# A GRU and an expert-choice layer on one core: units of the expert product twice as wide and in odd steps only, a block of the x products moved to even steps

## The chip, the core and the metric

The kernel runs on one core of one Trainium2 chip. The metric is the device time of one execution in microseconds; of several runs the median is taken. The profile is of one further execution of the same program.

## What is computed

A GRU runs over 256 steps on a batch of 16 with 512 channels. Its states are the tokens (16 x 256 = 4096) of an expert-choice layer: a router of 16 experts, a softmax, for each expert its 256 best tokens, and one weight matrix that all experts share. The result is added to `x`.

```python
def cell(h, x):
    gi = x @ W_ih + b_ih
    gh = h @ W_hh + b_hh
    i_r, i_z, i_n = jnp.split(gi, 3, axis=-1)
    h_r, h_z, h_n = jnp.split(gh, 3, axis=-1)
    r = jax.nn.sigmoid(i_r + h_r)
    z = jax.nn.sigmoid(i_z + h_z)
    n = jnp.tanh(i_n + r * h_n)
    return (1.0 - z) * n + z * h
# ffn over the states xf (4096 x 512), k = 4096 / 16 = 256
S = jax.nn.softmax(xf @ router_w + router_b, axis=-1)
G, idx = jax.lax.top_k(S.T, k)
out = jnp.einsum('ekh,hd->ekd', xf[idx], expert_w) + expert_b
y = zeros.at[idx].add(G[..., None] * out)
return x + y
```

Since the experts share a matrix, a token's output is its one row of `xf @ expert_w + expert_b` times the sum of the weights of those experts that chose it.

## The kernel before

**Tiling.** All matrix products are float32. TensorE is used as four strips of 32 columns: the 512 output channels are split over them (`tile_position=(0, 32 * j)`), and a loop over `j` issues four matmuls, one for each strip. Such a set of four is called a block here when it has 128 columns of the moving operand (32 channels x 4 chunks, or 128 channels of the expert matrix). In the trace each float32 matmul shows as two instructions, so a block is eight.

**The recurrence.** Loop `s` runs over the 256 steps; `p` is a pair of steps, `odd` the second of a pair, `g` a group of 8 steps and `c` the step in it. The order of instructions on all engines in this loop is the order in which the program writes them (a manual schedule). In a step TensorE does, in order:

1. `h_part` (L450 to L467): the products of the state with `W_hh`, for r and n over the first half of the channels, then over the second half, then for z. These wait for the state `hs`, whose two halves VectorE writes separately (L593). 12 blocks.
2. `x_part` (L436 to L448): the products of the pair after this one with `W_ih`, done for two steps at a time. For r and n together a matmul has 256 columns, for z 128. The even step does `k` 0 to 2 of r and n, the odd step `k` 3 of r and n and all four `k` of z. Each accumulates onto the bias that ScalarE has copied into the PSUM bank before.
3. An expert unit (L401 to L415): one block of one 128-column quarter of the expert product of an earlier group. There are 16 units in a group (4 quarters x 4 `k`), for the 15 `early_groups`; a counter lets one unit pass in each step from step 8 on. Or, in the first two steps of every fourth group (`apart`, steps 32 and 33, 64 and 65, up to 224 and 225), the router's `logits` of the four groups before (L336 to L351), into the right part of the bank `hn` of the next pair; the units left out follow in the step after.

Meanwhile ScalarE and VectorE work at the gates: sigmoid of r (L518), `t` = r x n part + i_n part (L568, L570), tanh (L572), sigmoid of z (L573), 32 x 32 transposes (L579, L582), and h = n + z (h - n) (L585, L590, L593).

**The bias copies of the next pair** are ScalarE's, in even steps. `preset_first` (L422) fills the bank `ra` right after r's sigmoid. `preset_rest` (L425) comes after z's sigmoid and fills `hn` (L426), in one pair of sixteen also clears the part for logits (L430), and then fills `zz` (L434).

**After the steps** TensorE still has the expert product of the 17 `late_groups`. It is cut into pieces by a generator, `late_parts` (L161 to L177), and `expert_for(n)` takes the next `n` of them wherever TensorE would wait: in the last two steps, after the last logits, in each of the 17 bits of the search for each expert's 256th largest weight (`by_bits`, L668: VectorE counts, a matmul adds up over partitions at L678, VectorE decides), and around what follows it. A piece is `late_part` (L133) over half of the 512 columns for one `k`, two blocks' worth; after the gate is known (`gated`) a piece is all 512 columns. What is left then is done in one go, and VectorE's `store` (L715) multiplies by the gate, adds `x` and sends the group out.

**Loads.** The weights come first on the queues of SyncE and ScalarE, the biases, the first `x` and `cond` on GpSimd's. `ewr` (expert and router matrix), `rb` (router bias, broadcast) and `eb` (expert bias, broadcast) follow on SyncE's (L296 to L299). `rb` is first read after the logits of step 33, `eb` in step 7.

Of the kernel before, what the change touches and what calls it, by code (L numbers as in the profile page):

```python
# [18 lines left out]
def kernel(  # L19
# [34 lines left out]
    nc = tc.nc  # L54
    B, T, D = x.shape
    E = router_w.shape[1]
    P = 128
    QD = 32
    KC = D // P
    TG = P // B  # L60
# [7 lines left out]
    HD = D // 2  # L68
    ewr = const.tile([P, KC, E + D], F32, name="ewr")
# [75 lines left out]
            )  # L145

    whole, halves_d = slice(0, D), [slice(0, HD), slice(HD, D)]

    late_items = [(g, whole) for g in late_groups[:-1]] + [(late_groups[-1], half) for half in halves_d]
    late = []  # L150
# [2 lines left out]
    gated = []  # L153
# [7 lines left out]
    def late_parts():  # L161
        for i, (g, cols) in enumerate(late_items):
            pe = late[0]
            for k in range(KC):

                for part in [cols] if gated or cols != whole else halves_d:
                    late_part(g, pe, k, part)
                    if k == KC - 1 and part.stop == cols.stop:
                        if i + 2 < len(late_items):
                            late_begin(ps_m if (i + 2) % 6 < 2 else late_pool[0])  # L170
                        late.pop(0)
                        late_done.append((g, cols))
                        if gated:
                            late_sums[g, cols.start] = pe
                        else:
                            nc.scalar.copy(wide(g), pe)
                    yield  # L177
# [4 lines left out]
    def expert_for(n):  # L182
        for _ in range(n):
            next(parts, None)


    with (
# [31 lines left out]
        def quadrant(j, m=QD):  # L219
            return slice(QD * j, QD * j + m)  # L220
# [44 lines left out]
        with tc.manual_schedule(engines={ET.SP, ET.Activation, ET.Pool}):  # L265
            def load_pairs(p, n, queue):

                for j in range(KC):
                    for i in range(n):
                        at = 2 * (p + i)  # L270
                        queue.dma_start(
                            out=xa0[quadrant(j), p + i, :],
                            in_=x[:, at : at + 2, j * P : (j + 1) * P].rearrange("b o d -> o b d"),
                        )

            for i, gate in enumerate((0, 2, 1)):
                load_rows(wih[:, :, i, :], w_ih[:, gate * D : (gate + 1) * D], "(p c) n -> p c n")
            for gate in (0, 2, 1):
                load_rows(whh[:, :, gate, :], w_hh[:, gate * D : (gate + 1) * D], "(c p) n -> p c n")

            for dst, src in (
                (b_raw[0:1], b_ih.rearrange("(o g d) -> o g d", o=1, d=D)),
                (b_raw[1:2], b_hh.rearrange("(o g d) -> o g d", o=1, d=D)),
                (b_n, b_hh[2 * D :].rearrange("(o d) -> o d", o=1)),
            ):
                nc.gpsimd.dma_start(out=dst, in_=src)
            load_pairs(0, 2, nc.gpsimd)
            nc.gpsimd.memset(c0, 0.0)
            for j in range(KC):
                nc.gpsimd.dma_start(  # L290
                    out=c0[QD * j : QD * j + B, :].rearrange("b (c i) -> b c i", c=KC), in_=columns(cond, j)
                )
            load_pairs(2, TG // 2 - 2, nc.sync)
            for j in range(KC):
                load_xa(1, xa1, j, (nc.sync, nc.sync))
            nc.sync.dma_start(out=ewr[:, :, E:], in_=expert_w.rearrange("(c p) n -> p c n", c=KC))  # L296
            nc.sync.dma_start(out=ewr[:, :, 0:E], in_=router_w.rearrange("(c p) n -> p c n", c=KC))
            nc.sync.dma_start(out=rb, in_=router_b.rearrange("(o e) -> o e", o=1).to_broadcast([P, E]))
            nc.sync.dma_start(out=eb, in_=expert_b.rearrange("(o d) -> o d", o=1).to_broadcast([P, D]))  # L299


# [51 lines left out]
        def last_logits(pl):  # L353

            j = KC - 1
            for k in range(KC):
                nc.tensor.matmul(
                    pl[quadrant(j, E)].rearrange("p (b t) -> p b t", t=TG)[:, :, TG - 1],
                    ewr[:, k, 0:E],
                    hs[:, k, slot(T), :],  # L360
                    start=False,
                    stop=(k == KC - 1),
                    tile_position=(0, QD * j),
                    skip_group_check=True,
                )

        def less_max(h, pl):
            l = gp.tile([P, KC, QD], F32, name="l")
# [26 lines left out]
        pes = {}  # L395
# [5 lines left out]
        def expert(g, unit):  # L401


            quarter, k = divmod(unit, KC)
            at = P * quarter
            for j in range(KC):
                nc.tensor.matmul(  # L407
                    pes[g][quadrant(j), at : at + P],
                    ht[:, g, k, quadrant(j)],
                    ewr[:, k, E + P * quarter : E + P * (quarter + 1)],  # L410
                    start=False,
                    stop=(k == KC - 1),
                    tile_position=(0, QD * j),
                    skip_group_check=True,
                )  # L415
# [9 lines left out]
        def preset_rest(p):  # L425
            nc.scalar.copy(hn[p % 2][:, 0:P], nb)  # L426


            if p % (KC * TG // 2) == TG + 1:
                nc.scalar.copy(  # L430
                    hn[p % 2][:, P:].rearrange("p (c e) -> p c e", e=QD),
                    zero.unsqueeze(1).to_broadcast([P, KC, QD]),
                )
            nc.scalar.copy(zz[p % 2], bias[:, 2, :])  # L434

        def x_part(p, k, z):  # L436
            g, pair = divmod(p, TG // 2)
            lhs = xT[g][:, pair, QD * k : QD * (k + 1)]
            for j in range(KC):
                q = quadrant(j)  # L440
                dst, rhs = (
                    (zz[p % 2][q], columns(wih[:, k, 2, :], j))
                    if z
                    else (ra[p % 2][q], columns(wih[:, k, 0:2, :].rearrange("p g d -> p (g d)"), j))
                )
                nc.tensor.matmul(  # L446
                    dst, lhs, rhs, start=False, stop=(k == KC - 1), tile_position=(0, QD * j), skip_group_check=True
                )  # L448
# [52 lines left out]

        with tc.manual_schedule(engines={ET.PE, ET.Activation, ET.DVE, ET.Pool, ET.SP}):
            seen = gp.tile([1, 8], F32, name="seen")
            units = [(g, unit) for g in early_groups for unit in range(16)]
            n_units = len(units)
            done = []
            for s in range(T):
# [20 lines left out]
                if 2 <= s < T - 2:  # L528
                    for k in range(3, KC) if odd else range(3):
                        x_part(p + 1, k, False)  # L530
                    if odd:
                        for k in range(KC):
                            x_part(p + 1, k, True)
                apart = g and g % KC == 0 and c < 2
                taken = done.pop(0) if done else None
                if apart:
                    logits(hn[(p + 1) % 2][:, P:], (2 * c, 2 * c + 1), range(g - KC, g))
                else:
                    while units and n_units - len(units) < s - TG + 1:
                        g_, unit = units.pop(0)  # L540
                        expert(g_, unit)
                        if unit == 15:
                            done += [(g_, 0), (g_, 1)]
                            break
                if s == T - 2:
# [1 line left out]
                if s == T - 1:  # L547
                    logits(hn[0][:, P:], range(KC), range(NG - 1, NG), slice(0, TG - 1))
                if s >= T - 2:
                    expert_for(1)  # L550

# [19 lines left out]
                nc.scalar.activation(zs, zz[p % 2], AF.Sigmoid)  # L573
                if not odd and 0 < p < T // 2 - 1:
                    preset_rest(p + 1)


                def turn_n(half):
# [57 lines left out]
            nc.vector.tensor_copy(  # L636
                ht[:, NG - 1, :, :].rearrange("p k (b t) -> p k b t", t=TG)[:, :, :, TG - 1], hs[:, :, slot(T), :]
            )
            expert_for(5)
            less_max(NG // KC - 1, hn[0][:, P:])  # L640
            for stage in range(4):
                softmax(slice(NG - KC, NG), stage)
# [2 lines left out]
    with (  # L645
# [85 lines left out]
        with tc.manual_schedule(engines={ET.PE, ET.Activation, ET.DVE}):  # L731
# [11 lines left out]
            nc.scalar.copy(by_block[:, 0 : KC - 1], ps[:, 0 : KC - 1, :].rearrange("p c (q i) -> p c q i", q=QG))  # L743
            nc.vector.tensor_copy(by_block[:, KC - 1], ps_last.rearrange("p (q i) -> p q i", q=QG))

            expert_for(2)
            counts = by_counts(HIGH - LOW + 1)
            top = by_bits(KNOWN, HIGH, LOW, counts, lambda bit: expert_for(3))


            nc.vector.scalar_tensor_tensor(at_least, sT, top.bitcast(F32), sT, ALU.is_le, ALU.mult)
# [6 lines left out]
                most.unsqueeze(1).to_broadcast([P, GH, NTOP]),  # L758
                ALU.mult,
            )  # L760
            expert_for(2)
            all_most = ps_n.tile([P, GH * NTOP], F32, name="all_most", tag="n")
            nc.tensor.matmul(all_most, same_f, spread.rearrange("p h n -> p (h n)"), start=True, stop=True)
            expert_for(3)
            room = above(counts)
            nc.vector.max(out=most, in_=all_most)
            kth = rt.tile([P, 1], F32, name="kth")
# [3 lines left out]
            for q in range(QG):  # L771
                part = slice(q * P, (q + 1) * P)
                nc.vector.scalar_tensor_tensor(at_least[:, part], sT[:, part], kth, sT[:, part], ALU.is_ge, ALU.mult)
                sum_weights(q, pg)
                if q % 2:
                    expert_for(1)
            gate = gate_of(pg)

            gated.append(True)
# [115 lines left out]
```

## Time and profile before

| | |
|---|---|
| median of 3 runs | 1161.14 us (1160.76 to 1162.51) |
| the profiled execution | 1161.04 us |
| its span, first to last instruction | 1159.2 us |
| granted TensorE clock, mean | 0.999 |
| TensorE busy | 1147.5 us, 99% |
| VectorE busy | 703.7 us, 61% |
| ScalarE busy | 343.4 us, 30% |
| first state product | 20.94 us |
| end of the last step | some 1087.8 us |
| gate ready, first store | some 1123.4 us |

In the rows of a timeline the first number is the start in us from the span's start, the second how long the row lasts; then the engine (PE TensorE's matmuls, PEld its weight loads, DVE VectorE, ACT ScalarE, POOL GpSimd, SP the queue of SyncE), the line of the kernel, the operation, what it writes and reads, the shape, and how many instructions are merged in the row. In brackets stands how long the engine was idle before, and what ended that.

### The profile page before, as it was taken

The numbers are of one execution on the slowest core, as the hardware profiler recorded it, in microseconds if no ns is written. First come the engines' busy times: TensorE is split into PE (matmuls) and PEld (weight loads), VectorE is DVE, ScalarE is ACT, GpSimd is POOL, SyncE is SP. The second block draws the span as 40 slices with busy tenths as digits, with TensorE's granted clock in tenths as the row PEclk, the third lists the DMA queues.
The fourth block names the chain that finished last, engine by engine and source line by source line (L and its number), as shares of the span: only waits on it lengthen the run. The fifth ranks groups of instructions, "written<-read, shape, count | busy, mean of one in ns | idle before, by whom it ended". The sixth has DMA issues, their size and how long they took to land. (4 is left out here: it accounts for less than half of the span.)

```text
span 1159.2 us, 79459 instructions
## 1 busy us (share of the span) xinstructions
PE 1147.5 (99%) x36065; PEld 1010.1 (87%) x36065; DVE 703.7 (61%) x4078; ACT 343.4 (30%) x1459; POOL 99.7 (9%) x412
## 2 busy tenths in 40 slices
PE   8999999999999999999999999999999999999998
PEld 5899999999999989999999999999999999989742
DVE  2656665666666656666665656666656666666675
ACT  1323323332233323333232323233232322343320
POOL 3000010000000000000000000000000000000000
PEclk9999999999999999999999999999999999999999
DMA  7200000000000000000000000000000000000017
GB/s 235 76 21 20 20 19 22 21 20 19 21 22 21 18 21 20 20 21 20 21 20 21 20 21 18 23 20 20 18 23 21 20 19 20 20 19 13 3 49 246
DMA packets 48855, 38.03 MB, mean 33 GB/s; under 512 B 7968, under 2 KB 40800, under 8 KB 48512
## 3 DMA queue, kind: packets, MB, share of 16 engines
q1 hardware_dynamic: 46272, 29.56, 8.7%
q8 instruction: 284, 4.65, 1.7%
q10 hardware_dynamic: 1632, 3.15, 0.8%
q14 instruction: 59, 0.48, 0.1%
q0 software_dynamic: 608, 0.19, 0.1%
HBM read 24.47 MB, written 8.39 MB: 28 GB/s over the span
## 5 line engine op out<-in xcount | busy, mean ns | idle before, releaser
L459 PE MATMUL gates<-whh,hs 128*16 128x128 f32 x24576 | 719.8, 273 | 3.4 <-DVE zT L582 1.2
L459 PEld LDWEIGHTS gates<-whh,hs 128*16 128x16 f32 x24576 | 672.4, 103 | 9.8 <-DVE hs L593 3.6
L446 PE MATMUL gates<-wih,xt 128*32 128x256 f32 (+1 forms) x8192 | 379.4, 326 | 0.8 <-DVE xt L256 0.7
L446 PEld LDWEIGHTS gates<-wih,xt 128*32 128x32 f32 x8192 | 245.1, 110 | 67.7 <-DVE xt L256 1.2
L518 ACT ACTIVATE r<-gates 128x128 f32<-128x128 f32 x256 | 71.0, 278 | 603.9 <-PE gates L459 603.9
L522 DVE COPY seen<-r 1x1 f32<-1x1 f32 x256 | 36.4, 142 | 326.0 <-ACT r L518 326.0
L572 ACT ACTIVATE t<-t 128x64 f32<-128x64 f32 x512 | 103.0, 248 | 132.7 <-DVE t L570 132.7
L579 DVE STREAM_TRANSPOSE nT<-t 128x64 f32<-128x64 f32 x512 | 100.2, 234 | 49.1 <-ACT t L572 49.1
L582 DVE STREAM_TRANSPOSE zT<-zs 128x64 f32<-128x64 f32 x512 | 121.6, 238 | 0.2 <-issue 0.2
L593 DVE TENSOR_TENSOR hs<-v,nT 128x32 f32<-128x32 f32 x512 | 101.7, 199 | 21.7
L590 DVE TENSOR_TENSOR v<-u,zT 128x32 f32<-128x32 f32 x512 | 104.5, 204 | 8.8
L407 PE MATMUL pe<-ewr,ht 128*32 128x128 f32 x1920 | 93.9, 273 | 0.0
L568 DVE TENSOR_TENSOR t<-r,gates 128x64 f32<-128x64 f32 x512 | 89.7, 217 | 1.2 <-PE gates L459 1.2
L570 DVE TENSOR_TENSOR t<-t,gates 128x64 f32<-128x64 f32 x512 | 88.6, 215 | 0.0
L585 DVE TENSOR_TENSOR u<-hs,nT 128x32 f32<-128x32 f32 x512 | 78.3, 153 | 0.0
L407 PEld LDWEIGHTS pe<-ewr,ht 128*32 128x32 f32 x1920 | 59.5, 110 | 19.4
L573 ACT ACTIVATE zs<-gates 128x128 f32<-128x128 f32 x256 | 71.0, 277 | 0.0
L137 PE MATMUL pe<-ewr,ht 128*32 128x256 f32 (+1 forms) x848 | 64.3, 442 | 0.0
L623 POOL COPY xa<-hs 32x1 f32<-32x1 f32 x120 | 21.3, 177 | 479.1 <-DVE hs L593 298.2
L331 POOL COPY ht<-hs 128x128 f32<-128x128 f32 (+1 forms) x128 | 46.9, 397 | 160.3 <-DVE hs L593 152.4
L247 POOL COPY xs<-hs 1x1 f32<-1x1 f32 x128 | 22.5, 176 | 335.4 <-DVE hs L593 330.7
L137 PEld LDWEIGHTS pe<-ewr,ht 128*32 128x32 f32 x848 | 26.0, 109 | 26.2 <-issue 17.4
(102 smaller groups left out, 321.2 us busy)
## 6 DMA issues: line engine op xcount, KB each, us to landing
xs<-in_x_dram SPq DMA_DIRECT2D x128, 64.0 KB
xa<-in_x_dram SPq DMA_DIRECT2D x248, 32.0 KB
out_dram<-xs SPq DMA_DIRECT2D x31, 256.0 KB
wih<-in_L_cond_W_ih_dram SPq DMA_DIRECT2D x3, 512.0 KB
wih<-in_L_cond_W_ih_dram ACTq DMA_DIRECT2D x3, 512.0 KB
whh<-in_L_cond_W_hh_dram SPq DMA_DIRECT2D x3, 512.0 KB
whh<-in_L_cond_W_hh_dram ACTq DMA_DIRECT2D x3, 512.0 KB
ewr<-in_L_ffn_expert_w_dram SPq DMA_DIRECT2D x1, 1024.0 KB
```

What stands on the lines that cost most here:

```text
L137: nc.tensor.matmul(pe[q, cols], ht[:, g, k, q], ewr[:, k, E:][:, cols], start=False, stop=(k == KC - 1), tile_position=(0, QD * j), skip_g ...
L407: nc.tensor.matmul(pes[g][quadrant(j), at : at + P], ht[:, g, k, quadrant(j)], ewr[:, k, E + P * quarter : E + P * (quarter + 1)], start=F ...
L446: nc.tensor.matmul(dst, lhs, rhs, start=False, stop=(k == KC - 1), tile_position=(0, QD * j), skip_group_check=True)
L459: nc.tensor.matmul(dst[quadrant(j, m)], lhs, columns(whh[:, k, gate_, :], j), start=False, stop=(k == KC - 1), tile_position=(0, QD * j), ...
L568: nc.vector.tensor_tensor(t[half], r[:, cols], hn[p % 2][:, cols], ALU.mult)
L570: nc.vector.tensor_tensor(t[half], t[half], ra[p % 2][:, 1, cols], ALU.add)
L572: nc.scalar.activation(t[half], t[half], AF.Tanh)
L579: nc.vector.transpose(nT[half], t[half])
L582: nc.vector.transpose(zT[half], zs[:, halves[half][1]])
L585: nc.vector.tensor_tensor(u[half], hs[:, halves[half][2], slot(s), :], of_step(nT[half], odd), ALU.subtract)
L590: nc.vector.tensor_tensor(v[half], u[half], of_step(zT[half], odd), ALU.mult)
L593: nc.vector.tensor_tensor(hs[:, halves[half][2], slot(s + 1), :], v[half], of_step(nT[half], odd), ALU.add)
```

## The change

Five things are changed.

1. `expert` takes 256 columns instead of 128, so a group has 8 units, and the counter lets one pass in every second step, an odd one (or in step 34, 66 and so on, where one is made up for).
2. The z product of `k` = 0 for the next pair moves from the odd step to the even one. It is issued after `preset_rest`, so behind the expert unit or the logits of that step.
3. Before the gate is known, `late_parts` yields quarters of 128 columns instead of halves of 256. The counts of `expert_for` are doubled nearly everywhere.
4. Two more quarters are taken early: one between the second and third `k` of the last logits, and five instead of four before the search.
5. The load of `rb` is issued by GpSimd, after `cond`, instead of by SyncE.

```diff
+    quarters = [slice(P * i, P * (i + 1)) for i in range(KC)]
...
-                for part in [cols] if gated or cols != whole else halves_d:
+                for part in [cols] if gated or cols != whole else quarters:
...
-            nc.sync.dma_start(out=rb, in_=router_b.rearrange("(o e) -> o e", o=1).to_broadcast([P, E]))
+            nc.gpsimd.dma_start(out=rb, in_=router_b.rearrange("(o e) -> o e", o=1).to_broadcast([P, E]))
...
@@ last_logits, after the matmul of each k
+                if k == KC // 2 - 1:
+                    expert_for(1)
...
@@ expert(g, unit)
-            quarter, k = divmod(unit, KC)
-            at = P * quarter
+            half, k = divmod(unit, KC)
+            at = HD * half
             for j in range(KC):
                 nc.tensor.matmul(
-                    pes[g][quadrant(j), at : at + P],
+                    pes[g][quadrant(j), at : at + HD],
                     ht[:, g, k, quadrant(j)],
-                    ewr[:, k, E + P * quarter : E + P * (quarter + 1)],
+                    ewr[:, k, E + at : E + at + HD],
...
@@ the loop over the steps
-            units = [(g, unit) for g in early_groups for unit in range(16)]
+            units = [(g, unit) for g in early_groups for unit in range(2 * KC)]
...
                     if odd:
-                        for k in range(KC):
+                        for k in range(1, KC):
                             x_part(p + 1, k, True)
...
-                    while units and n_units - len(units) < s - TG + 1:
+                    while units and n_units - len(units) < (s - TG + 1) // 2:
                         g_, unit = units.pop(0)
                         expert(g_, unit)
-                        if unit == 15:
+                        if unit == 2 * KC - 1:
...
                 if s >= T - 2:
-                    expert_for(1)
+                    expert_for(2)
...
                 if not odd and 0 < p < T // 2 - 1:
                     preset_rest(p + 1)
+                    x_part(p + 1, 0, True)
...
@@ after the steps
-            expert_for(5)
+            expert_for(10)
...
-            expert_for(2)
+            expert_for(5)
             counts = by_counts(HIGH - LOW + 1)
-            top = by_bits(KNOWN, HIGH, LOW, counts, lambda bit: expert_for(3))
+            top = by_bits(KNOWN, HIGH, LOW, counts, lambda bit: expert_for(6))
...
-            expert_for(2)
+            expert_for(4)
...
-            expert_for(3)
+            expert_for(6)
...
                 if q % 2:
-                    expert_for(1)
+                    expert_for(2)
```

## The prediction, made before the changed kernel was run

> **What bounds the kernel now.** I read the page first. Its engine rows say which engine has no room left.
>
> ```profile
> PE 1147.5 (99%) x36065; PEld 1010.1 (87%) x36065; DVE 703.7 (61%) x4078; ACT 343.4 (30%) x1459; POOL 99.7 (9%) x412
> ```
>
> PE is busy for 99% of the span, but ends of matmuls are modelled, so this alone proves nothing. The second view is therefore the timeline of one ordinary pair of steps, an odd one (from 500.01 us) and the even one after it (from 504.15).
>
> ```profile
> 500.01 2.80 PE L459 MATMUL gates<-whh,hs 128*32 128x128 f32 x96
> 503.70 0.19 DVE L593 TENSOR_TENSOR hs<-v,nT 128x32 f32<-128x32 f32 x1
> 504.15 2.80 PE L459 MATMUL gates<-whh,hs 128*16 128x128 f32 x96
> 506.77 1.48 PE L446 MATMUL gates<-wih,xt 128*32 128x256 f32 x24
> 507.39 0.27 ACT L434 COPY gates<-bias 128x128 f32<-128x128 f32 x1
> 508.07 0.40 PE L407 MATMUL pe<-ewr,ht 128*32 128x128 f32 x8
> ```
>
> Four matmuls on the four column strips start within 20 ns and form a "round". The 96 h matmuls are 24 rounds in 506.77 - 504.15 = 2.62 us, 0.109 each. The six rounds of 256 columns take 1.30, about 0.216 each (single start times in the trace: 109.2 and 215.8 ns). A pair of steps is nothing but such rounds: the even step starts last 4.133 us and the odd ones 4.143, and 24 + 2 rounds of 109.2 and 6 of 215.8 make 4.134. The state is ready early: its first half is written at 503.89, the matmul that reads it starts at 504.15, and about 0.15 us of that is slack. So the recurrence is TensorE bound. What counts is rounds, and any time at which PE stands still.
>
> Third, the steps that have no expert unit (2 to 7 and 248 to 253).
>
> ```profile
> 1071.15 2.81 PE L459 MATMUL gates<-whh,hs 128*16 128x128 f32 x96
> 1075.10 2.56 PEld L459 LDWEIGHTS gates<-whh,hs 128*32 128x32 f32 x96 [0.32 <-DVE hs L593]
> 1079.06 2.81 PE L459 MATMUL gates<-whh,hs 128*16 128x128 f32 x96
> ```
>
> These last 3.95 and 3.96 us and wait for DVE: here the chain r, t, tanh, nT, hs is the bound, and PE has about 0.18 us to spare.
>
> Fourth, a step with logits (step 96, an even one, and its successors). ScalarE's waits name one that the ordinary steps lack, and the timeline shows it.
>
> ```profile
> ACT gates L426 <- PE gates L343: 10.4, 7, 1.5
> ```
>
> ```profile
> 424.21 0.62 PE L343 MATMUL gates<-ht,ewr 128*16 128x128 f32 x16
> 424.64 2.80 PE L459 MATMUL gates<-whh,hs 128*32 128x128 f32 x96
> 424.92 0.27 ACT L426 COPY gates<-nb 128x128 f32<-128x128 f32 x1 [1.48 <-PE gates L343]
> 425.12 0.27 ACT L434 COPY gates<-bias 128x128 f32<-128x128 f32 x1
> 429.00 3.03 PE L459 MATMUL gates<-whh,hs 128*16 128x128 f32 x96
> 429.28 0.32 DVE L369 STREAM_TRANSPOSE l<-gates 128x128 f32<-128x128 f32 x1
> 429.65 2.10 PEld L459 LDWEIGHTS gates<-whh,hs 128*16 128x16 f32 x80 [0.31 <-DVE l L369]
> ```
>
> The logits write into the bank `hn` of the next pair, so the copy of `nb` into that bank (L426) waits for them, and the copy into `zz` (L434) stands behind it on ScalarE: done at 425.39. Today nobody needs it before the odd step's z products, after 427.6. In ordinary steps the same copy ends at 507.66. The last two lines show a second fact: at 429.44 the n matmuls wait for DVE, and the r matmuls behind them, whose state was written at 429.13, do not pass: PE stands still.
>
> Last, the end of the kernel.
>
> ```profile
> 1094.15 1.50 PE L137 MATMUL pe<-ewr,ht 128*32 128x256 f32 x24
> 1095.32 0.09 DVE L663 DVE_READ_ACCUMULATOR ge<-sT,cand 128x1 f16 x1
> 1095.59 0.18 PE L678 MATMUL bank<-cnt,same_h 128*128 128x1 f16 x1
> 1123.03 19.95 PE L137 MATMUL pe<-ewr,ht 128*32 128x256 f32 x192
> ```
>
> A bit of the search lasts 1.54 us. Its pieces fill the wait and the count matmul starts some 0.1 us after DVE is ready, because the pieces end late. From 1123.03 on PE works without a gap at the late groups, and the last stores follow it.
>
> **The change part by part.**
>
> *Merged units.* 240 units of 128 columns (2 rounds each) become 120 of 256 (2 rounds each): 480 x 109.2 becomes 240 x 215.8, 0.6 us less. The Trainium skill disagrees on the size ("TensorE: Matmul & The Clock Gate", Back-to-back issue gap): it gives a lone gap of N/2.4 + 2.5 ns, but some 81 ns instead of 56 for 128 columns in a stream with weight loads, 25 ns more per matmul. By that the 240 rounds saved would be worth 6 us and would pay for everything below. Here a 256-column round costs 215.8 and two of 128 cost 218.4, with weight loads in both, so the saving is 2.5 ns a round; I take 0.6.
>
> *The z block in ordinary even steps.* Two rounds go from the odd step to the even one, and the expert unit goes the other way: 26 + 6 rounds, as before. The odd step also keeps its length. The wait added is for the `zz` copy: done at 507.66, and PE reaches the block at 508.07, so it costs 0, with 0.35 us of cover. Behind it on PE stand the next step's h matmuls, so all of a delay beyond this cover would be paid, 119 times.
>
> *The z block in the seven even steps with logits.* No expert unit stands in them; the block follows the logits at once. PE is ready for it at 424.64 (the time of the next round). Its bank gets its bias only at 425.39: logits end 424.83, L426 starts 0.09 later, L434 ends 0.47 after that. For the release of PE I add 0.05, as in the DVE rows (L369 ends 429.60, load at 429.65). PE stands still from 424.64 to 425.44, 0.80 us; the next h matmuls are queued behind, DVE and ScalarE wait for those, and nothing later wins it back since PE is the bound. 7 x 0.80 = 5.6 us. Bounds: 0.65 if the release is free and the copies close up, 0.95 with a slow release: 4.6 to 6.7. That an engine pulls only weight loads ahead and keeps matmuls in order is also what the skill says (same page, What happens when you issue a matmul); the row at 429.65 is nearer and agrees.
>
> *The odd step with logits* loses its two rounds, which shift to the even one. So the next step starts 0.22 sooner after its chain: hs ends 0.35 into it instead of 0.13, L369 starts at 0.38 instead of 0.28, and the n matmuls, due at 0.44, wait 0.31 instead of 0.21. 7 x 0.1 = 0.65 us (0 to 1.0).
>
> *Even steps without units.* In steps 2, 4, 6, 248, 250, 252 the block comes on top: 24 + 2 rounds and 6 wide ones make 4.133 instead of 3.95 (4.007 in step 248). The odd steps that lose it are bound by the chain and win nothing. 5 x 0.185 + 0.126 = 1.05 us (0.8 to 1.2).
>
> *Quarter pieces.* A half piece is 2 rounds of 215.8, two quarters are 4 of 109.2: 5 ns more each. In each of 16 bits 6 quarters cost 15 ns more: 0.24; the 10, 6 and 4 before the gate 0.04. The last matmul of the four strips is shorter (273 ns instead of 379, the L459 and L446 rows), but it starts as much later, so nothing is won there (bounds per bit: 0.1 less if the count matmul is released by the start of the last round, 0.03 more). Two quarters fill gaps: in the last logits PE waits 0.5 us for the second half of the state, where 0.22 fit; before the first bit the fifth quarter ends just before the count is there. They take half a piece, 0.43 us, off the continuous stretch behind 1123.03. Net -0.15 us (-2 to +0.4).
>
> *rb on POOL.* One SP issue less (0.50 at L298), one of about 0.53 more on POOL at 12.2 us (the L290 rows), behind `cond` and ahead of the masks. The masks' POOL work then ends near 13.8; DVE takes it up at 17.8. rb is first read in step 33. SP sends `eb` 0.55 sooner, which no one awaits before step 7. I take 0 (-0.3 to +0.5: its 128 packets meet the weight loads, and the 1.1 us without an instruction at 42.4 may shift).
>
> *Sum.* 5.6 + 0.65 + 1.05 - 0.6 - 0.15 = +6.55 us. The profiled execution took 1161.04 us (span 1159.2 and 1.8 around it), which makes 1167.6; the median of the runs is 0.1 higher: **1167.7 us**, +0.56%.
>
> **The rivals.**
>
> *Faster: exposed weight loads go.* If each 128-column unit round waits for its load (the loads are busy 110 ns, nearly a round of 109.2), merging saves far more than 2.5 ns. From 39 ns a round (9.4 us over 240) the change ends faster; at half a load, 55 ns, it gives 13.2 and 1161.0 + 7.15 - 13.2 = 1155 us. Against it: 256 columns take 215.8, so the columns themselves cost 107 to 108 ns per 128 and no such time is hidden in the 109.2. Chance 0.03.
>
> *No stall at the logits.* If the `zz` copy is out before the logits are (or PE has other work there), only 1.05 + 0.65 - 0.6 - 0.15 = 0.95 remain: 1162.1 us, no difference. Against it: L434 is issued after L426 on ScalarE, and L426 waited for L343 in all seven. Chance 0.05.
>
> *The wait costs in every even step.* If the `zz` copy takes up the 0.35 us of cover and 0.1 more, 119 steps add 12 us: 1180. Nothing in the even steps' ScalarE work moves, so 0.04.
>
> *As summed* (PE waits in seven steps): 0.88, of its own between 1165.8 and 1169.6.
>
> **How the numbers follow.** A measurement of this kernel can tell about 0.2% (2.3 us) from no change. The likeliest case lies beyond that at both ends. Its range comes from the terms: stalls +-1.0, tail -1.9 to +0.5, start +-0.5, which rarely all fall on one side, and runs that differ by 1 us. It holds the time 8 times in 10 with the rivals left outside. Slower: 0.88 + 0.04, and 0.01 for less likely slow ones; no difference 0.04; faster 0.03.
>
> **What would show it.** In the profile after, ScalarE's `nb` copy still waits for the logits seven times, and a new wait of PE for the `zz` copy of about 0.8 us stands in exactly those steps, with the h matmuls 1.0 us behind the logits. Steps 250 and 252 last 4.13; ordinary pairs 8.27. A bit lasts 1.555. It would be wrong if the steps at 96, 128 and so on are not longer by 0.8, if the ordinary even steps show PE waiting for ScalarE, or if a merged unit takes clearly less than 0.43 us.

## The result, and the profile after

| | before | after |
|---|---|---|
| median of 5 runs, us | 1161.22 (1160.76 to 1162.51) | 1167.33 (1167.13 to 1170.03) |
| profiled execution, us | 1161.04 | 1167.15 |
| its span, us | 1159.2 | 1165.4 |
| its granted clock | 0.999 | 0.999 |

The ratio is 1.0053, with a 95% interval of 1.0043 to 1.0064: 6.1 us slower, where 6.55 us were forecast.

TensorE is still the bound. From the profile's page of after, the engines' busy time and the rows of the x products and of the merged units:

```profile
PE 1149.6 (99%) x35649; PEld 998.4 (86%) x35649; DVE 703.9 (60%) x4078; ACT 343.4 (29%) x1459; POOL 100.7 (9%) x413
...
L449 PE MATMUL gates<-wih,xt 128*32 128x256 f32 (+1 forms) x8192 | 382.2, 326 | 5.7 <-ACT gates L437 4.3
...
L410 PE MATMUL pe<-ewr,ht 128*32 128x256 f32 x960 | 73.8, 379 | 0.0
```

PE has 416 matmuls fewer than before (the units 960 fewer, the quarter pieces 544 more) and yet 2.1 us more of busy time; the rest of the longer span, 4.1 us, is idle time. The units are there in their new shape (960 = 240 rounds of four strips), and nothing idles ahead of them. The row of the x products names the place of the idle time: 5.7 us ahead of them, 4.3 of it ended by the copy at L437. The same row of before:

```profile
L446 PE MATMUL gates<-wih,xt 128*32 128x256 f32 (+1 forms) x8192 | 379.4, 326 | 0.8 <-DVE xt L256 0.7
```

How often it waits, and what the copy itself waits for, stands in the list of waits (waiting engine, tile and line, releaser, total us, times, longest):

```profile
ACT gates L429 <- PE gates L344: 10.4, 7, 1.5
...
PE gates L449 <- ACT gates L437: 4.3, 7, 0.6
```

The first line stood before too, word for word but for its line numbers: ScalarE's copy of `nb` waits for the logits seven times. The second is new: seven times TensorE waits for ScalarE's `zz` copy. The list counts 0.61 us for each, but that is only the part in which PE ran nothing at all; what the path lost is read from the starts. One of these steps, step 96, in the timeline of after (start, duration, engine, line, tiles; in brackets the idle time before it and its releaser):

```profile
426.55 0.62 PE L344 MATMUL gates<-ht,ewr 128*16 128x128 f32 x16
...
427.26 0.27 ACT L429 COPY gates<-nb 128x128 f32<-128x128 f32 x1 [1.48 <-PE gates L344]
...
427.47 0.26 ACT L437 COPY gates<-bias 128x128 f32<-128x128 f32 x1
...
427.78 0.43 PE L449 MATMUL gates<-wih,xt 128*32 128x128 f32 x8 [0.61 <-ACT gates L437]
...
428.02 2.80 PE L462 MATMUL gates<-whh,hs 128*32 128x128 f32 x96
```

The logits take four rounds of 109 ns, so PE could have gone on at 426.99 (426.55 + 0.44). The `nb` copy starts 0.09 after the logits end (at 427.17), the `zz` copy follows it 0.21 later and ends at 427.73, and the z block starts 0.05 after that, at 427.78. That is a standstill of 0.79 us; from the lengths of the seven pairs it is 0.82 each. The h matmuls of the next step come only behind the z block, at 428.02.

An ordinary pair of steps, in the timeline of after:

```profile
502.24 0.27 ACT L437 COPY gates<-bias 128x128 f32<-128x128 f32 x1
503.13 2.80 PE L462 MATMUL gates<-whh,hs 128*32 128x128 f32 x96
...
506.83 0.61 PE L410 MATMUL pe<-ewr,ht 128*32 128x256 f32 x8
507.27 2.80 PE L462 MATMUL gates<-whh,hs 128*16 128x128 f32 x96
```

The `zz` copy is done at 502.51. The z block, whose two rounds are the last before 503.13, starts at 502.91: 0.4 us later, and after the 0.05 of the release 0.35 us of cover are left. The merged unit goes from 506.83 to 507.27, 0.44 us for its two wide rounds, and the pair lasts 4.14 + 4.14 as before. Even steps without a unit, by contrast, got longer (timeline, steps 248 to 250):

```profile
1077.79 2.81 PE L462 MATMUL gates<-whh,hs 128*16 128x128 f32 x96
...
1081.93 2.80 PE L462 MATMUL gates<-whh,hs 128*32 128x128 f32 x96
...
1085.87 2.81 PE L462 MATMUL gates<-whh,hs 128*16 128x128 f32 x96
```

Step 248 takes 4.13 (4.007 before) and step 249 takes 3.94 (3.96 before): the block was added on one side, and only 0.02 came back on the other. At the end of the kernel, from the timeline:

```profile
1113.42 0.18 PE L682 MATMUL bank<-cnt,same_h 128*128 128x1 f16 x1
...
1114.97 0.18 PE L682 MATMUL bank<-cnt,same_h 128*128 128x1 f16 x1
...
1130.21 19.53 PE L137 MATMUL pe<-ewr,ht 128*32 128x128 f32 x192
...
1149.75 0.09 DVE L667 DVE_READ_ACCUMULATOR ge<-sT,kth 128x1 f16 x1
...
1149.89 0.16 PE L792 MATMUL n<-cnt,same_h 128*128 128x1 f16 x1
```

A bit of the search, from one count matmul to the next, takes 1.55 us (1.54 before). The continuous stretch behind it lasts 19.53 instead of 19.95, one half piece less. But then the matmul that checks the count (L792) stands in PE's queue until VectorE's count is read out at 1149.84, and half of the saving is gone.

The sum over the whole span, from the starts of the steps in both traces:

| stretch | change, us |
|---|---|
| start to the first state product | +0.33 |
| seven even steps with logits (4.351 to 5.389), the odd ones after them (4.362 to 4.143) | +5.73 |
| six even steps without units | +1.11 |
| all other steps, step 240 left out | -0.61 |
| step 240 | +0.24 |
| last step to the gate | +0.38 |
| gate to the last store's sum | -0.23 |
| from there to the end of the span | -0.80 |
| span, 1159.2 to 1165.4 | +6.16 |

### The profile page after: what moved, and what is told of

Its sections match the earlier page's. It is cut to its first block, busy times and chain, and to the rows that moved or that the text cites. A ratio compares the mean times of both kernels' runs of the same rounds, so it can differ in the third digit from the quotient of the medians.

```text
span 1165.4 us, 78630 instructions
## 1 busy us (share of the span) xinstructions
PE 1149.6 (99%) x35649; PEld 998.4 (86%) x35649; DVE 703.9 (60%) x4078; ACT 343.4 (29%) x1459; POOL 100.7 (9%) x413
## 5 line engine op out<-in xcount | busy, mean ns | idle before, releaser
L449 PEld LDWEIGHTS gates<-wih,xt 128*32 128x32 f32 x8192 | 248.9, 110 | 95.7 <-ACT gates L437 8.5
L410 PE MATMUL pe<-ewr,ht 128*32 128x256 f32 x960 | 73.8, 379 | 0.0
L137 PE MATMUL pe<-ewr,ht 128*32 128x128 f32 (+2 forms) x1392 | 64.9, 334 | 0.0
L137 PEld LDWEIGHTS pe<-ewr,ht 128*32 128x32 f32 x1392 | 38.6, 110 | 19.0 <-issue 17.3
L426 ACT COPY gates<-bias 128x256 f32<-128x256 f32 x126 | 47.6, 378 | 0.0
```

The source lines that it names most:

```text
L137: nc.tensor.matmul(pe[q, cols], ht[:, g, k, q], ewr[:, k, E:][:, cols], start=False, stop=(k == KC - 1), tile_position=(0, QD * j), skip_g ...
L410: nc.tensor.matmul(pes[g][quadrant(j), at : at + HD], ht[:, g, k, quadrant(j)], ewr[:, k, E + at : E + at + HD], start=False, stop=(k == K ...
L449: nc.tensor.matmul(dst, lhs, rhs, start=False, stop=(k == KC - 1), tile_position=(0, QD * j), skip_group_check=True)
```

## The experiments

The theory: the loss is made in the seven even steps with logits, by one wait, because the `zz` copy stands behind an `nb` copy that waits for the logits. Rivals: the steps without units, the tail or the moved load of `rb` carry it; or the narrow rounds had hidden weight-load time, and more than 2.5 ns each is won. Each median stands beside that of the kernel before, taken on the same chip. The ratio is estimated from the single runs, so it can differ from the quotient of the two medians, here by up to 0.04%.

### The block stays where it was, in the seven pairs alone (after, one condition)

```diff
-                        for k in range(1, KC):
+                        for k in range(1 if not (g and g % KC == 0 and c < 2) else 0, KC):
...
-                    x_part(p + 1, 0, True)
+                    if not (g and g % KC == 0 and c < 2):
+                        x_part(p + 1, 0, True)
```

> The changed kernel, but in the seven pairs of steps with logits (32, 64 ... 224) the z block of k = 0 stays in the odd step. Theory (TensorE waits there for the zz copy, which stands behind the logits on ScalarE): the even steps with logits go back from 5.39 to 4.35 us and the odd ones from 4.14 to 4.36, 5.7 us less: ratio to before about 1.0004, 1161.6 us. Rival (the 6 us come from something spread over the ordinary steps, such as the 256-column units or the z block in all even steps): at most 1 us less, 1.0045.

Measured: 1161.52 against 1161.08, ratio 1.0006 [0.9998, 1.0014]. The even logits steps are back at 4.351 and the odd ones at 4.362. All of the slowdown that can be measured came with the block in these seven pairs.

### Two copies swapped (after)

```diff
         def preset_rest(p):
+            nc.scalar.copy(zz[p % 2], bias[:, 2, :])
             nc.scalar.copy(hn[p % 2][:, 0:P], nb)
...
-            nc.scalar.copy(zz[p % 2], bias[:, 2, :])
```

> The changed kernel with the order of two ScalarE copies turned round: zz before nb, so that the zz copy no longer stands behind the copy that waits for the logits. The z block stays in the even steps with logits. Theory: the wait of 0.61 us at the matmul (0.82 us in the starts) goes, 5.7 us less, about 1161.6 us, ratio 1.0004. Rival (it is not ScalarE's order: a block right behind the logits costs that much in itself, for instance since the logits' matmuls must drain): no gain, 1.005.

Measured: 1161.38 against 1161.08, ratio 1.0004 [0.9996, 1.0012]. The block stays in the even steps; only the order of two copies on ScalarE is changed. Step 96 in the timeline of this kernel:

```profile
423.76 0.27 ACT L429 COPY gates<-bias 128x128 f32<-128x128 f32 x1
...
424.63 0.62 PE L344 MATMUL gates<-ht,ewr 128*16 128x128 f32 x16
...
425.07 0.40 PE L447 MATMUL gates<-wih,xt 128*32 128x128 f32 x8
...
425.35 0.27 ACT L430 COPY gates<-nb 128x128 f32<-128x128 f32 x1 [1.31 <-PE gates L344]
```

The `zz` copy is out before the logits have begun, and the z block starts 0.44 after them, four rounds later, with no gap. The `nb` copy waits as ever, and nothing that TensorE waits for stands behind it. The even logits step takes 4.570: its old 4.351 and the block's 0.22, which the odd step gives back. So it is the place in ScalarE's queue that costs, not the moved work.

### The wait alone (before, block moved in the seven pairs only)

```diff
-                        for k in range(KC):
+                        for k in range(1 if g and g % KC == 0 and c < 2 else 0, KC):
...
                     preset_rest(p + 1)
+                    if g and g % KC == 0 and c < 2:
+                        x_part(p + 1, 0, True)
```

> The kernel before, with the z block of k = 0 moved into the even step in the seven pairs of steps with logits alone. Nothing else changed. Theory: all of the stall and nothing else, 7 x 0.81 = 5.7 us more, 1166.9 us, ratio 1.0049. Rival (the stall needs the wider units or comes with the other parts): under 2 us more.

Measured: 1167.32 against 1161.08, ratio 1.0054 [1.0041, 1.0068]. Its list of waits has the line of after, with this kernel's line numbers:

```profile
PE gates L446 <- ACT gates L434: 4.3, 7, 0.6
```

Seven moved blocks alone give the time of the whole change; in the trace of this kernel the seven pairs account for 5.73 us, as in after. The cause is therefore shown from three sides: it goes when the block goes, it goes when the block no longer waits, and it comes with nothing else changed.

### The rest of the change without its costs (after, copies swapped, blocks moved only in steps with units, rb on SP)

```diff
-                        for k in range(1, KC):
+                        for k in range(1 if TG <= s < T - TG else 0, KC):
...
-                    x_part(p + 1, 0, True)
+                    if TG <= s < T - TG:
+                        x_part(p + 1, 0, True)
```

> The changed kernel mended at each place where the trace shows it lose: zz copied before nb, the z block moved only in the steps that have expert units (8 to 247), rb loaded on SyncE's queue again. What stays is the wider units, the moved block and the quarter pieces. Theory: 0.6 us from the units and 0.15 to 0.6 from the pieces: 1160.1 to 1160.5 us, ratio 0.9992 (no difference that a measurement here can tell). Rival (weight loads of 128-column units were exposed and merging gains much more, hidden until now by the stall): 1155 us, 0.995.

Measured: 1160.25 against 1161.08, ratio 0.9992 [0.9984, 1.0000]. The merged units and the quarter pieces together bring 0.8 us, by the interval at most 1.9. That is in line with 2.5 ns a round (0.6 us); a gain of 6 us, as 25 ns a round would make it, lies far outside. No kernel had the merged units alone, but the traces show their share: an ordinary odd step lasts 4.138 us instead of 4.143, 5 ns for two wide rounds in place of four narrow ones, and ordinary even steps last 4.133 in both.

### Parts done alone on before: quarter pieces, rb on POOL, the block in pairs without units

```diff
-                for part in [cols] if gated or cols != whole else halves_d:
+                for part in [cols] if gated or cols != whole else quarters:
...
-            top = by_bits(KNOWN, HIGH, LOW, counts, lambda bit: expert_for(3))
+            top = by_bits(KNOWN, HIGH, LOW, counts, lambda bit: expert_for(6))
```

> The kernel before with the quarter pieces alone (parts 3 and 4 of the change). By the prediction's sum -0.15 us (+0.28 until the gate, -0.43 behind it), 1161.0 us; by the one profile of the changed kernel, in which the stretch from the last step's start to the end is 0.6 us shorter, -0.6. Rival: none of it counts, since the last stores and not TensorE set the end: +0.3 us or 0. These lie close together; the stretches of the profile tell more than the ratio.

Quarter pieces (with all counts doubled as in the change): 1161.67 against 1161.38, ratio 0.9998 [0.9990, 1.0007]. From the last step to the gate 0.27 is lost, behind it 0.23 is won: nothing is left.

```diff
-            nc.sync.dma_start(out=rb, in_=router_b.rearrange("(o e) -> o e", o=1).to_broadcast([P, E]))
+            nc.gpsimd.dma_start(out=rb, in_=router_b.rearrange("(o e) -> o e", o=1).to_broadcast([P, E]))
```

> The kernel before with rb loaded by GpSimd (part 5 alone). By the prediction 0. By the profile of the changed kernel, whose first state product starts at 21.27 instead of 20.94 us with the first x transposed 0.33 later, +0.33 us. Rival: the start differs by as much between executions of one kernel, and the load has no part in it: first state product anywhere between 20.9 and 21.3.

The load of `rb`: 1161.17 against 1161.38, ratio 0.9997 [0.9989, 1.0006]. No difference shows in the total, though two stretches of its trace moved (see the last section).

```diff
-                        for k in range(KC):
+                        for k in range(1 if not TG <= s < T - TG else 0, KC):
...
                     preset_rest(p + 1)
+                    if not TG <= s < T - TG:
+                        x_part(p + 1, 0, True)
```

> The kernel before with the z block of k = 0 moved to the even step only where no expert unit stands (pairs from step 2 and from step 248 on). Theory: those six even steps become bound by TensorE, 4.13 us instead of 3.95, and the odd ones, bound by the chain, win nothing: +1.1 us, 1162.3 us, ratio 1.0009. Rival: the odd steps give it back: 0.

Pairs without units: 1161.95 against 1161.38, ratio 1.0007 [0.9999, 1.0016]. Those even steps take 4.13 to 4.14 in its trace, as in after, so the lengthening is there; the 0.6 to 0.8 us in the total are not told from no change, since the interval includes 1.

### How far the cover of the ordinary even steps reaches (after, the copy made two or three times, outside the logits pairs)

```diff
-            nc.scalar.copy(zz[p % 2], bias[:, 2, :])
+            for _ in range(3 if (p - 1) % 16 else 1):
+                nc.scalar.copy(zz[p % 2], bias[:, 2, :])
```

The computed values stay the same; the copy only ends later, by 0.30 us per repetition in the trace. The kernel with three copies (the diff) ran first, and the expectation for two (2 in place of 3) rests on it.

> The changed kernel with the zz copy made twice in all pairs but those with logits. In e8_cover3 two more copies came 0.295 us apart and made the ordinary even steps 0.27 us longer, so the cover is 2 x 0.295 - 0.27 = 0.32 us. One more copy, 0.295, lies just inside it. Theory (a threshold): no difference from the changed kernel but in the eight pairs in which the logits' half is cleared too, where 0.05 us is left and 0.2 to 0.25 each is paid: 1167.3 + 2 = 1169.3 us. Rival (every delay of the copy is paid in proportion): half of e8_cover3's loss, 1183 us.

> The changed kernel with the zz copy made three times instead of once in all pairs but those with logits (the same values, so nothing else differs). A test of the cover in the ordinary even steps: in the trace the z block starts 0.406 us after the copy has ended, and a wait ends 0.051 after it, so 0.355 us are free. Two more copies take 2 x 0.20 us if they follow as close as zz follows nb today, up to 2 x 0.33 if each waits for the one before. Theory: 0.05 to 0.3 us of stall in some 119 steps, +6 to +36 us, 1173 to 1203 us. Rival (TensorE finds other work, or the wait is taken up by slack later in the step): no more than the changed kernel, 1167.3.

Twice: 1169.24 against 1161.02, ratio 1.0068 [1.0054, 1.0082], 1.9 us above after. Three times: 1199.66 against 1161.38, ratio 1.0330 [1.0316, 1.0344], 32 us above after. The lists of waits of the two kernels, twice first, then three times, show weight loads waiting in both:

```profile
PEld gates L450 <- ACT gates L438: 36.4, 119, 0.9
```

```profile
PEld gates L450 <- ACT gates L438: 70.1, 119, 0.9
```

Of the 119 waits seven are those of the logits steps, the same 6.3 us as in after; eight fall in the pairs in which ScalarE also clears the logits half of the bank; 104 are of ordinary steps. One of these in the timeline of each kernel, twice first:

```profile
508.35 2.80 PE L463 MATMUL gates<-whh,hs 128*16 128x128 f32 x96
...
512.21 0.19 PEld L450 LDWEIGHTS gates<-wih,xt 128*32 128x32 f32 x8 [0.24 <-ACT gates L438]
...
512.48 2.80 PE L463 MATMUL gates<-whh,hs 128*32 128x128 f32 x96
```

```profile
513.07 2.80 PE L463 MATMUL gates<-whh,hs 128*16 128x128 f32 x96
...
517.23 0.16 PEld L450 LDWEIGHTS gates<-wih,xt 128*32 128x32 f32 x8 [0.55 <-ACT gates L438]
...
517.47 2.80 PE L463 MATMUL gates<-whh,hs 128*32 128x128 f32 x96
```

A row of waits does not tell the price. In the first kernel the loads of the 104 ordinary steps wait 25.7 us in all, and it costs nothing: only loads waited, they still came in time, and these steps last 4.13 as before. What is paid, some 2 us, comes from the pairs with the clearing, where the second copy finds the cover used up: step 48 takes 4.41 instead of 4.13, and six others are as much longer (the eighth, step 240, was 0.24 longer in after already). In the second kernel the loads of the ordinary steps wait 57.0 us, and each of the steps takes 4.405, 0.27 more: two additional copies are 0.60, so 0.33 had been free, where 0.35 were forecast. The 104 steps make 28 us of the 32, the pairs with the clearing, 0.58 longer each but step 240, 4.4; the other steps together were 0.6 shorter in this execution, nearly all of it in step 5. The seven steps behind the logits, which the prediction's 119 include, pay nothing. Cover is a threshold: 0.30 of delay cost nothing in the ordinary steps, 0.60 cost what lies above 0.33.

### A version faster than both (the mended kernel, other order of products in the step after the logits)

```diff
+                if g and g % KC == 0 and c == 2:
+                    order = [("r", first), ("r", second), ("n", first), ("n", second)]
+                else:
+                    order = [(gate, ks) for ks in (first, second) for gate in "rn"]
+                for gate, ks in order:
+                    h_part(s, gate, ks)
-                for ks in (first, second):
-                    h_part(s, "r", ks)
-                    h_part(s, "n", ks)
```

> The mended kernel (e4_mend) and one thing more: in the step after the logits (34, 66 ... 226) the h products go r, r, n, n instead of r, n, r, n over the two halves. Today the n matmuls there wait for VectorE to read the logits out of their bank, and the r matmuls queued behind stand still with them: 0.21 us in the starts. The second half of r needs the second half of the state, which is there. Theory: those steps go from 4.79 to 4.57 us, 7 x 0.21 = 1.5 us less than e4_mend, 1158.8 us, ratio 0.998. Rival (the chain through r, t and tanh sets the step once TensorE doesn't wait, or n comes too late for t): 0 to 0.5 us less.

Measured: 1158.92 against 1161.02, ratio 0.9978 [0.9968, 0.9988], 0.2% faster than before. The n products wait for VectorE to read the logits out of their bank. With all r products ahead of them PE has work meanwhile (timeline of this kernel, step 98):

```profile
428.96 2.80 PE L460 MATMUL gates<-whh,hs 128*16 128x128 f32 x96
...
429.23 0.32 DVE L372 STREAM_TRANSPOSE l<-gates 128x128 f32<-128x128 f32 x1
...
433.52 2.69 PE L460 MATMUL gates<-whh,hs 128*32 128x128 f32 x92
```

The 96 products now take 2.80, where they took 3.03 before, and the step 4.565 instead of 4.787: 7 x 0.22 = 1.55 us. This gain is not the change's; it mends a standstill that before had too.

A last edit put one piece of the late product (all 512 columns, since the gate is known there) ahead of the matmul that checks the count:

```diff
                 if step == 1:
+                    expert_for(1)
                     n = ps_n.tile([P, 1], F32, name="n", tag="n")
```

> As e9_rrnn, and near the end one piece of the late product ahead of the matmul that adds up the check counts, which in the changed kernel's profile waits 0.2 us for VectorE's count and so loses half of what the early pieces won. Theory: 0.2 us less from the gate to the last store (30.34 to 30.14 us in the profile), too little for the ratio. Rival (the check then comes too late for VectorE, or the last DMAs set the end): the stretch stays at 30.3.

Measured: 1158.90 against 1161.02, ratio 0.9981 [0.9974, 0.9989]. From the gate to the last store it takes 30.14 instead of 30.35, as expected, but the total did not move. 0.2 us of 1159 cannot be told in these runs, whose times lie up to 1.7 us apart.

## Why the prediction was right, point by point

- **The stall at the logits** carried the forecast and carries the result. Its chain (logits end, 0.09 to the `nb` copy, 0.47 to the end of the `zz` copy, 0.05 to PE) came out link by link: 0.80 forecast per step, 0.82 measured, 5.6 against 5.73 us. The rival without a stall had the right remedy but not this kernel: it holds only with the copies swapped. That no later matmul passes the one that waits, as the prediction has it, agrees with these seven standstills. Strict program order over all four strips the traces do not show: before, a first matmul of L137 starts at 1082.37, ahead of three of the logits (L343) at 1082.46 that the program has in front of it (by the kernel, on the one strip that these logits leave free). No run here shows a matmul pass one that waits for another engine.
- **The step after the odd logits step** is the mis-sized term: 0.65 us forecast, nothing measured (4.787, was 4.793 in step 98). The failing step was "L369 starts at 0.38 instead of 0.28". It rested on the end of the state's row. The timeline of after:

```profile
432.17 3.02 PE L462 MATMUL gates<-whh,hs 128*16 128x128 f32 x96
432.32 0.19 DVE L597 TENSOR_TENSOR hs<-v,nT 128x32 f32<-128x32 f32 x1
432.44 0.32 DVE L372 STREAM_TRANSPOSE l<-gates 128x128 f32<-128x128 f32 x1
432.81 2.10 PEld L462 LDWEIGHTS gates<-whh,hs 128*16 128x16 f32 x80 [0.31 <-DVE l L372]
```

  The state's row ends at 432.51, 0.34 into the step, as forecast. But the transpose starts at 432.44, before that end: VectorE's rows overlap by 0.07. It starts 0.09 after the logits end (431.73 + 0.62 = 432.35), so the logits release it, at the same place in the step as before, and the n matmuls wait 0.31 as they did.
- **Even steps without units**: 1.05 forecast, 1.11 measured in the step lengths; the total of the kernel with this part alone does not tell it from nothing. The prediction's reading that PE has 0.18 us to spare there is wrong, though its sum does not use it: 24 rounds of 109.2 ns and six of 215.8 are 3.92 us of a step of 3.95, so 0.03 is free, and that is why a block of 0.22 costs 0.19. The odd steps gave back 0.10 in all, where nothing was forecast.
- **Merged units and the block in ordinary even steps**: 0.6 us less forecast. In the trace the ordinary odd steps are shorter by 0.50 in all; the mended kernel is 0.8 us faster. The z block costs nothing there, behind 0.33 us of cover. From the figures of the Trainium skill ("TensorE: Matmul & The Clock Gate", Back-to-back issue gap) the estimate was 6 us, with 25 ns more for each matmul; the measurement, 5 ns for two rounds saved, decides for the small gap, and the rival of exposed weight loads (1155 us) falls with it.
- **Quarter pieces**: a bit takes 1.55 as forecast; up to the gate +0.38 against +0.28, behind it -0.23 against -0.43. The stretch lost its half piece as forecast, but the count check's wait took back 0.2. Net +0.15 in place of -0.15.
- **What was not forecast**: step 240 +0.24, the start +0.33, the end of the span -0.80. They cancel to about -0.2. So that the total is so close (6.1 for 6.55) is partly luck: the other misses, of both signs, made up some 0.3 of the 0.65 us too much behind the logits. The cause and its size do not rest on that.
- **The wait in every even step** (1180 us) did not come; the kernel with three copies shows how it looks once the cover is used up.

## What to carry to other kernels

When a block is moved onto an engine that is the bound, look at who releases it, and then at what stands ahead of the releaser in its own queue, in the special steps above all: here 104 ordinary even steps had 0.33 us to spare, and seven with logits cost nearly the whole 6 us. A copy that others wait for belongs ahead of a copy that itself waits; that one swap gave the 6 us back. Hidden time is a threshold, and a row of waits is no price: in the 104 steps 25.7 us of waiting weight loads cost nothing, and 57.0 cost 28.

## What the runs showed of the hardware that was not expected

Two ScalarE copies of 128 columns start 0.20 us apart where one goes to `hn` and the other to `zz`, in either order (the swapped kernel too), and 0.30 us apart where both go to the same bank: `zz` written twice, or `nb` and the cleared half, which lie side by side in `hn`. That it is the bank and not something else that these pairs share was not tested.

In step 240 of after, VectorE pauses ahead of the last operation of the state (timeline, VectorE alone):

```profile
1031.28 0.19 DVE L594 TENSOR_TENSOR v<-u,zT 128x32 f32<-128x32 f32 x1
1031.95 0.19 DVE L597 TENSOR_TENSOR hs<-v,nT 128x32 f32<-128x32 f32 x1 [0.47 <-DVE v L594]
```

The step takes 4.375 instead of 4.134. All four profiles with `rb` on POOL's queue and the `zz` copy made once show this (4.375 to 4.379), and none with `rb` on SP's (4.133 to 4.134). With `rb` on SP, before pauses in the same step too, 0.21 us at a place where it costs nothing. From the last store to the end of the span the kernels with `rb` on POOL take 4.55 to 4.89 us, those with it on SP 5.09 to 5.51. Why a load at the start of the kernel does either stays open; in the total (ratio 0.9997) neither shows. The first state product starts anywhere between 20.91 and 21.49 over all profiles, and step 5, the one near 42 us, lasts between 4.62 and 6.05, with no link to an edit that these single profiles would show. Both spreads are as large as several terms of the sum.
